# Attention groups kept together on TensorE, a block's outputs finished in the next block, and a new order in the last pair

## The chip, the cores and the metric

The kernel runs on one core of a Trainium2 chip. The core has a matrix engine (TensorE, in profiles PE, with its weight loads as PEld), a vector engine (VectorE, DVE), a scalar engine (ScalarE, ACT), GpSimd (POOL) and SyncE (SP), which here only issues DMAs. Each engine runs its own list of instructions in order, and they meet through semaphores. TensorE writes to a small memory of eight banks, PSUM, from which VectorE and ScalarE read; the rest lies in SBUF. The metric is the time of one execution on the device in microseconds. The figure for a kernel is the median of its timed runs.

## The reference, cut to what matters

The input x is 32 x 64 x 512, the context has the same shape, and all is float32. The first layer is cross attention in which the 64 rows are the channels: a row of 512 is cut into 8 heads of 64, the projections are 64 x 64 matrices that act on the channel axis, and the scores are 64 x 64 for each batch entry and head.

```python
x = x + attention(layernorm(x), ctx, ctx)      # per head: softmax(q k^T / 8) v, then Wo and bo
h = layernorm(x)
gate = silu(h @ dequant(gate_w))               # 512 -> 1792
up   = h @ dequant(up_w)
x = x + (gate * up) @ dequant(down_w)          # 1792 -> 512
```

`dequant` subtracts an integer zero point and multiplies by a scale, both per group of 128 rows and per column. All three weights are integers from 0 to 15.

## The kernel before

Two batch entries side by side make a "pair" of 128 rows, so there are 16 pairs. Four pairs make a block of 512 columns for the feed-forward part; there are four blocks, numbered 0 to 3 (t). Attention works on sets of two pairs, named after their first pair: 0, 2, 4, ... 14.

Feed-forward. The activations are kept transposed, as a high and a low part (hTh, hTl). For each of 14 columns of weights (f), `gate_up` (L615) multiplies four groups g of gate and up weights with both parts into PSUM tiles pg and pu (L624). ScalarE rescales pg and pu between groups (L634), applies SiLU at the last (L637), VectorE forms h (L640), and GpSimd splits it into hh and hl (L650, L651). `down` (L656) multiplies hh and hl with the down weights (L669, L672), and VectorE adds the product into one of four y tiles (L682); a block's first column is copied to y by ScalarE instead (L680). So a column takes 16 matmuls up and 8 down, each with 512 columns. Two lanes of `gate_up` run side by side.

Attention. The class `Attention` (L337) has one method a step: k, v and q projections, scores, the highest of a row, less (subtract), exp, sums, divide, turn (weights times Wo), weigh (times v), residual, and then a second layer norm and flip (transposition for the feed-forward part). Steps k, v, q, scores, turn and weigh are groups of 64 small TensorE products (64 x 64, in four quarters of the array) or, for v, of 16. Each group writes to a tile of two PSUM banks, of which there is one for all (`two_banks`, L872), shared with the transposes of the finishing steps.

Order. A Python loop (L895) emits the program in rounds, 28 to a block and six more at the end. Each round emits a step of lane 0, the attention steps listed for that round in ROUND_STEPS (L576), a `down` step, a step of lane 1, weights still to be dequantised (or sums of squares for a check of the inputs), finishing steps, and a `down` step. Attention of block t+1 is emitted in the rounds of block t. A planner then gives each engine its order: among the instructions that it holds ready it takes the one that was emitted first, that is, of the best priority. Three means bend this. `tc.manual_schedule` keeps the order of a group's instructions on an engine, but others may come between them. `tc.issue_after(ins)` queues instructions behind a given one on its engine, without waiting for its end. `tc.high_priority()` gives what is emitted inside it the priority of the program's start. The start-up part (the list START) is in a written order on all engines.

Finishing. `finish(t)` (L686) has four steps for a block: load the attention result of two pairs from DRAM into the single tile r (L691); transpose their y on TensorE (L696), add (L699) and store (L700); then the same for the other two pairs. Before the change it is created at round LAG = 6 of block t+1 and advanced in rounds 7, 9 and 11, and for the fourth step in round 5 of the block after; for block 2 that is the very end of the loop. `finish_last` (L703) does the four pairs of block 3 after the loop: 16 transposes (L711), three adds on VectorE (L715), for the last pair a copy on ScalarE (L718) and an add on GpSimd (L719), and stores issued in turn by SP and ScalarE (L720). Then every engine reads a flag (L930) and branches: where the check of the inputs failed, a slow general path would follow. The flag is written by VectorE (L749) about twelve rounds before the end.

Of the kernel before, what the change touches and what calls it, by code (L numbers as in the profile page):

```python
# [9 lines left out]
F32 = mybir.dt.float32  # L10
# [16 lines left out]
def kernel(  # L27
# [41 lines left out]
    nc = tc.nc  # L69
    B, D, L = x.shape  # L70
    I = gate_w.shape[1]
    P = 128
# [3 lines left out]
    LC = L // P  # L76
    NPAIR = B // 2
    PB = 4
    NBLK = NPAIR // PB
    TB = PB * P  # L80
    SET = 2
# [4 lines left out]
    o_rows = out.rearrange("(n b) d l -> (b d) n l", b=2)  # L86
# [7 lines left out]
    flag = keep.tile([1, 1], I32, tag="flag", name="flag")  # L94
    ident = keep.tile([P, P], F32, tag="ident", name="ident")
# [18 lines left out]
    with ExitStack() as fast:  # L114
# [96 lines left out]
        def proj(m: int, b: int) -> bass.AP:  # L211
            return w_T[ts(b, D), (m - b) % 4, :]
# [106 lines left out]
        def top_steps():  # L319
# [9 lines left out]
            for piece in pieces:  # L329
# [3 lines left out]
                nc.gpsimd.tensor_tensor(total[:, :n], total[:, :n], square[:, :n], ALU.add)  # L333
                yield


        class Attention:  # L337

# [64 lines left out]
            def heads(self, part: str, m: int, name: str):  # L403
                pp, quarters = self.quarters(name)
                src = self.by_head(part)
                with self.in_order():
                    for c, b, h in quarters:
                        nc.tensor.matmul(
                            pp[ts(h, HD), b, c, :],
                            src[ts(b, D), c, h, :],  # L410
                            proj(m, b),
                            start=True,
                            stop=True,
                        )
                return pp

            def with_bias(self, part: str, pp: bass.AP, m: int):
# [17 lines left out]
            def v(self):  # L435
                self.pv, _ = self.quarters("pv")
                src = self.by_head("c")
                with self.in_order():
                    for i in range(self.n):
                        for h in range(2):  # L440
                            for b in range(2):
                                nc.tensor.matmul(
                                    self.pv[ts(h, D), b, ts(i, KT), :],
                                    proj(WV, b),
                                    src[ts(b, D), ts(i, KT), h, :],
                                    start=True,
                                    stop=True,
                                )

            def v_out(self):  # L450
                nc.scalar.activation(self.by_bank("v"), self.pv, AF.Identity, bias=bvo[:, 0:1])


            def scores(self):
                self.pss, quarters = self.quarters("pss")
                qT, kT = self.by_bank("q_e"), self.by_bank("k_eT")
                with self.in_order():
                    for c, b, h in quarters:
                        nc.tensor.matmul(
                            self.pss[ts(b, D), h, c, :],  # L460
                            qT[ts(h, HD), b, c, :],
                            kT[ts(h, HD), b, c, :],
                            start=True,
                            stop=True,
                        )

            def highest(self):
                n = self.n * KT
# [31 lines left out]
            def turn(self):  # L500
                self.pe, quarters = self.quarters("pe")
                e = self.by_head("q_e")
                with self.in_order():
                    for c, b, h in quarters:
                        nc.tensor.matmul(
                            self.pe[ts(h, D), b, c, :],
                            e[ts(b, D), c, h, :],
                            proj(WO, b),
                            start=True,
                            stop=True,  # L510
                        )

            def turn_out(self):
                nc.scalar.copy(self.by_bank("k_eT"), self.pe)

            def weigh(self):
                self.po, quarters = self.quarters("po")
                eT, vv = self.by_bank("k_eT"), self.by_bank("v")
                with self.in_order():
                    for c, b, h in quarters:  # L520
                        nc.tensor.matmul(
                            self.po[ts(b, D), h, c, :],
                            eT[ts(h, D), b, c, :],
                            vv[ts(h, D), b, c, :],
                            start=True,
                            stop=True,
                        )

            def residual(self):
                x_heads = self.by_head(self.x)  # L530
# [53 lines left out]
        FINISH_AT = 7, 11  # L584
# [27 lines left out]
        h_hi, h_lo, y_sb, pd_two = {}, {}, {}, {}  # L612
# [73 lines left out]
        def finish(t: int):  # L686

            for a in range(0, PB, SET):
                p = t * PB + a
                r = rows.tile([P, SET, L], F32, tag="r", name=f"r_{p}")  # L690
                nc.sync.dma_start(r, x1_dram[:, p : p + SET, :])  # L691
# [7 lines left out]
                nc.vector.tensor_tensor(r, py, r, ALU.add)  # L699
                nc.sync.dma_start(o_rows[:, p : p + SET, :], r)  # L700
                yield

        def finish_last():  # L703

            t = NBLK - 1
            py = [ps_gu.tile([P, CW], F32, tag="gu", name=f"py_last_{i}") for i in range(2)]
            two = two_banks("py_last")
            py += [two[:, 0, :], two[:, 1, :]]
            for l in range(LC):
                for i in range(PB):  # L710
                    nc.tensor.transpose(py[i][:, ts(l, P)], y_sb[t, l][:, ts(i, P)], ident)  # L711
            for i in range(PB):
                r = xs[(t * PB + i) // SET][:, i % SET, :]
                if i < PB - 1:
                    nc.vector.tensor_tensor(r, py[i], r, ALU.add)  # L715
                else:
                    y = hid.tile([P, TB], F32, tag="g", name="y_last", bufs=2)
                    nc.scalar.copy(y, py[i])  # L718
                    nc.gpsimd.tensor_tensor(r, y, r, ALU.add)  # L719
                (nc.scalar if i % 2 else nc.sync).dma_start(o_rows[:, t * PB + i, :], r)  # L720


        def check_bounds():
# [57 lines left out]
        with (  # L781
# [9 lines left out]
            for p in range(PB):  # L791
                j, i = divmod(p, SET)
# [74 lines left out]
        hid = fast.enter_context(tc.tile_pool(name="hid", bufs=3))  # L867
# [22 lines left out]
        LAG = 6  # L890
# [3 lines left out]
        with ExitStack():  # L894
            for r in range(NBLK * ROUNDS + LAG):  # L895
                t, k = divmod(r, ROUNDS)
                if k == 0:
                    attend = attention_steps(t + 1) if t + 1 < NBLK else iter(())
                if k == LAG and t > 0:
                    finishing = finish(t - 1)  # L900
                next(lanes[0], done)
                advance(attend)
                if r >= LAG:
                    advance(downs)
                if r >= 2:
# [24 lines left out]
    with tc.If(nc.values_load(flag, min_val=0, max_val=1) != 0), ExitStack() as slow:  # L930
# [108 lines left out]
```

## Time and profile before

| | us |
|---|---|
| median of 3 timed runs | 449.24 (447.51 to 450.96) |
| profiled execution | 446.75 |
| its span, first to last instruction | 444.6 |
| TensorE busy in the span | 411.4 (93%) |
| VectorE, ScalarE, GpSimd busy | 327.6, 307.0, 280.3 |
| mean granted TensorE clock | 0.989 |

The profile is of one execution. In its rows a line such as "L624" is a line of the kernel. The names of tiles stand as out<-in, without the numbers of their buffers; "x64" is a count. "idle before <- releaser" tells how long the engine had nothing to do before the row and whose semaphore ended that. Matmuls overlap, so the sum of their lengths is more than the time they take; their starts are the better measure. A "q" behind an engine's name means its sequencer: it issues a DMA, reads a register or waits.

### The profile page before, as it was taken

Reading aid. Unit: us, or ns where it says so; the run is one execution under the profiler, and the core shown is the slowest. Engines: PE = TensorE matmul, PEld = TensorE weight load, DVE = VectorE, ACT = ScalarE, POOL = GpSimd, SP = SyncE. Lnnn points to the kernel's source line nnn. Section 1 sums busy time; section 2 is a strip of 40 time slices with the busy share of each in tenths; the row PEclk is TensorE's granted clock in tenths of the full one; section 3 lists DMA queues with packets and bytes.
Section 4 is the critical chain, followed back from the end, with each engine's and each line's share of the span. In section 5 each row is a group of like instructions: output and inputs, shape, how many; then the busy total and the mean of one; then the engine's idle time right before and its main releaser. Section 6 shows DMA issues by size and latency. Waiting matters only on the chain.

```text
span 444.6 us, 10356 instructions
## 1 busy us (share of the span) xinstructions
PE 411.4 (93%) x4191; PEld 316.2 (71%) x4191; DVE 327.6 (74%) x514; ACT 307.0 (69%) x469; POOL 280.3 (63%) x292
## 2 busy tenths in 40 slices
PE   3878979989989999999999999989999999999991
PEld 3656657757768776887788786867778888887871
DVE  4998486896779873895779884896868645668673
ACT  2243886855957589676978589666788787777750
POOL 4384876746844546575778668665787878883311
PEclk9999998999999999999999999999999999999996
DMA  6299585295011200411010102400010012100004
GB/s 210 61 304 369 190 278 150 92 276 177 2 49 49 96 2 0 129 64 50 0 49 1 50 20 77 137 7 1 1 49 2 1 61 83 47 1 0 1 2 149
DMA packets 20912, 36.55 MB, mean 82 GB/s; under 512 B 1832, under 2 KB 7416, under 8 KB 20856
## 3 DMA queue, kind: packets, MB, share of 16 engines
q1 hardware_dynamic: 14056, 24.20, 16.0%
q0 software_dynamic: 6192, 11.01, 8.4%
q8 instruction: 35, 0.57, 0.5%
q10 hardware_dynamic: 608, 0.59, 0.4%
q14 instruction: 21, 0.17, 0.1%
HBM read 27.37 MB, written 8.42 MB: 81 GB/s over the span
## 4 chain that ended last, share of the span: by engine, by line
PE 55%; POOL 17%; issue 11%; DVE 10%; ACT 2%; DMA 2%; ACTq 0%; POOLq 0%; DVEq 0%
PE pu L624 15%; PE pg L624 14%; PE pd L669 8%; PE pd L672 7%; POOL hl L651 5%; POOL squares L333 4%; POOL squares L331 3%; POOL hh L650 2%; DVE y L682 2%; DVE xn_set L112 1%; POOL q_e_set L496 1%; DMA w_nat<-in_L_xattn_Wo_dram 1%; DMA z<-z_dram 1%; DVE q_e_set L473 1%; DVE nd L301 1%
## 5 line engine op out<-in xcount | busy, mean ns | idle before, releaser
L682 DVE SCALAR_TENSOR_TENSOR y<-pd,s_all,y 128x512 f32<-128x512 f32 x204 | 150.5, 743 | 45.8 <-PE pd L672 43.2
L634 ACT ACTIVATE pg<-pg,s_q 128x512 f32<-128x512 f32 x168 | 111.5, 665 | 74.4 <-PE pg L624 73.0
L634 ACT ACTIVATE pu<-pu,s_q 128x512 f32<-128x512 f32 x168 | 110.7, 659 | 5.8 <-PE pu L624 5.6
L669 PE MATMUL pd<-hh,nd 128*128 128x512 f32 x224 | 93.4, 417 | 4.1 <-DVE y L678 2.0
L650 POOL CAST hh<-h 128x512 fp32r<-128x512 f32 x55 | 35.7, 649 | 97.6 <-DVE h L640 93.4
L624 PE MATMUL pg<-hTh,ng 128*128 128x512 f32 x224 | 90.4, 403 | 2.5 <-DVE hTl L567 1.6
L624 PE MATMUL pu<-hTh,nu 128*128 128x512 f32 x224 | 90.5, 404 | 2.3 <-POOL nu L310 2.0
L624 PE MATMUL pu<-hTl,nu 128*128 128x512 f32 x224 | 89.5, 399 | 0.0
L624 PE MATMUL pg<-hTl,ng 128*128 128x512 f32 x224 | 89.0, 397 | 0.0
L672 PE MATMUL pd<-hl,nd 128*128 128x512 f32 x224 | 88.8, 397 | 0.0
L651 POOL TENSOR_TENSOR hl<-h,hh 128x512 fp32r<-128x512 f32 x55 | 72.1, 1311 | 4.3
L640 DVE SCALAR_TENSOR_TENSOR h<-pu,s_all,g 128x512 f32<-128x512 f32 x56 | 41.8, 747 | 29.5 <-ACT g L637 21.4
L333 POOL TENSOR_TENSOR squares<-squares 128x512 f32<-128x512 f32 (+1 forms) x46 | 55.0, 1196 | 1.6
L669 PEld LDWEIGHTS pd<-hh,nd 128*128 128x128 f32 x224 | 42.0, 188 | 19.8 <-DVE y L682 4.9
L624 PEld LDWEIGHTS pg<-hTh,ng 128*128 128x128 f32 x224 | 42.3, 189 | 15.2 <-issue 3.2
L624 PEld LDWEIGHTS pu<-hTh,nu 128*128 128x128 f32 x224 | 42.3, 189 | 14.2 <-POOL nu L310 2.5
L624 PEld LDWEIGHTS pu<-hTl,nu 128*128 128x128 f32 x224 | 42.4, 189 | 9.8 <-issue 0.4
L624 PEld LDWEIGHTS pg<-hTl,ng 128*128 128x128 f32 x224 | 42.2, 189 | 9.5
L637 ACT ACTIVATE g<-pg,s_all 128x512 f32<-128x512 f32 x56 | 38.7, 692 | 14.0 <-PE pg L624 12.4
L672 PEld LDWEIGHTS pd<-hl,nd 128*128 128x128 f32 x224 | 42.3, 189 | 7.9
L310 POOL TENSOR_TENSOR ng<-ng,z 128x512 fp32r<-128x512 f32 (+1 forms) x16 | 16.5, 1039 | 3.4 <-DMA z<-z_dram 3.4
L310 POOL TENSOR_TENSOR nu<-nu,z 128x512 fp32r<-128x512 f32 (+1 forms) x16 | 16.9, 1057 | 2.1 <-DMA nu<-in_L_ffn_up_w_dram 2.0
(293 smaller groups left out, 473.2 us busy)
## 6 DMA issues: line engine op xcount, KB each, us to landing
c_set<-in_ctx_dram SPq DMA_DIRECT2D x6, 512.0 KB
x<-in_x_dram SPq DMA_DIRECT2D x6, 512.0 KB
z<-z_dram SPq DMA_DIRECT2D x6, 512.0 KB
ng<-in_L_ffn_gate_w_dram POOLq DMA_DIRECT2D x3, 1024.0 KB, 6.7
nu<-in_L_ffn_up_w_dram POOLq DMA_DIRECT2D x3, 1024.0 KB, 9.0
x_dram<-x SPq DMA_DIRECT2D x6, 512.0 KB
r<-x_dram SPq DMA_DIRECT2D x6, 512.0 KB
out_dram<-r SPq DMA_DIRECT2D x6, 512.0 KB
```

Source lines behind the costliest of these rows:

```text
L310: nc.gpsimd.tensor_tensor(piece, piece.bitcast(F32), z16[:, m, g, :], ALU.subtract)
L331: nc.gpsimd.tensor_tensor(square[:, :n], piece, piece, ALU.mult)
L333: nc.gpsimd.tensor_tensor(total[:, :n], total[:, :n], square[:, :n], ALU.add)
L624: nc.tensor.matmul(acc, w[:, g, ts(f, P)], half[:, g, :], start=(g == 0 and half is hi), stop=(g == KT - 1 and half is lo), skip_group_che ...
L634: nc.scalar.activation(acc, acc, AF.Copy, scale=by)
L637: nc.scalar.activation(g_sb, acc, AF.Silu, scale=by)
L640: ins = nc.vector.scalar_tensor_tensor(h_sb, acc, by, g_sb, ALU.mult, ALU.mult)
L650: nc.gpsimd.tensor_copy(hh, h_sb)
L651: ins = nc.gpsimd.tensor_tensor(hl, h_sb, hh.bitcast(F32), ALU.subtract)
L669: nc.tensor.matmul(pd, w, h_hi[t, f], start=(t, f) != LAST, stop=False, skip_group_check=True)
L672: nc.tensor.matmul(pd, w, h_lo[t, f], start=False, stop=True, skip_group_check=True)
L682: ins = nc.vector.scalar_tensor_tensor(y, pd, by, y, ALU.mult, ALU.add)
```

## The change

It has three parts. First, a new context `in_one_piece` takes the place of the plain written order in the six group steps of Attention, for sets of two pairs, and is put around the transposes of `finish`. It keeps the order as before, and after the group's first product it raises the priority of the rest. Second, `finish(t-1)` is created at round 5 rather than 6, so its four steps fall in rounds 5, 7, 9 and 11 of one block. Third, in `finish_last` ScalarE's copy of the last pair is emitted ahead of the adds, and the stores that ScalarE issues are queued behind it; the read of the flag is emitted before `finish_last`, and what `finish_last` gives ScalarE and GpSimd is queued behind those engines' reads.

```diff
+        @contextmanager
+        def in_one_piece(rush: bool = True):
+            with tc.manual_schedule(engines={mybir.EngineType.PE}), ExitStack() as ahead:
+                yield lambda: ahead.enter_context(tc.high_priority()) if rush else None
...
             def in_order(self):
-                return tc.manual_schedule(engines={mybir.EngineType.PE})
+                return in_one_piece(self.n > 1)
...
-                with self.in_order():
+                with self.in_order() as first_taken:
                     for c, b, h in quarters:
                         nc.tensor.matmul(
...
                         )
+                        first_taken()
...
                 py = two_banks(f"py_{p}")
-                for i in range(SET):
-                    for l in range(LC):
-                        nc.tensor.transpose(
-                            py[:, i, ts(l, P)], y_sb[t, l][:, ts(a + i, P)], ident
-                        )
+                with in_one_piece() as first_taken:
+                    for i in range(SET):
+                        for l in range(LC):
+                            nc.tensor.transpose(
+                                py[:, i, ts(l, P)], y_sb[t, l][:, ts(a + i, P)], ident
+                            )
+                            first_taken()
...
+            y = hid.tile([P, TB], F32, tag="g", name="y_last", bufs=2)
+            copied = nc.scalar.copy(y, py[PB - 1])
             for i in range(PB):
                 r = xs[(t * PB + i) // SET][:, i % SET, :]
                 if i < PB - 1:
                     nc.vector.tensor_tensor(r, py[i], r, ALU.add)
                 else:
-                    y = hid.tile([P, TB], F32, tag="g", name="y_last", bufs=2)
-                    nc.scalar.copy(y, py[i])
                     nc.gpsimd.tensor_tensor(r, y, r, ALU.add)
-                (nc.scalar if i % 2 else nc.sync).dma_start(o_rows[:, t * PB + i, :], r)
+                with tc.issue_after(copied.ins):
+                    (nc.scalar if i % 2 else nc.sync).dma_start(o_rows[:, t * PB + i, :], r)
...
-                if k == LAG and t > 0:
+                if k == FINISH_AT[0] - 2 and t > 0:
                     finishing = finish(t - 1)
...
-        finish_last()
-    with tc.If(nc.values_load(flag, min_val=0, max_val=1) != 0), ExitStack() as slow:
+        n_traced = len(nc.cur_bb.bb.instructions)
+        other = nc.values_load(flag, min_val=0, max_val=1)
+        with ExitStack() as behind:
+            for ins in nc.cur_bb.bb.instructions[n_traced:]:
+                if ins.engine in (mybir.EngineType.Activation, mybir.EngineType.Pool):
+                    behind.enter_context(tc.issue_after(ins))
+            finish_last()
+    with tc.If(other != 0), ExitStack() as slow:
```

More of the change, by code (lines that the diff above doesn't have):

```diff
@@ L437, in v @@
                 src = self.by_head("c")
-                with self.in_order():
+                with self.in_order() as first_taken:
                     for i in range(self.n):
@@ L456, in scores @@
                 qT, kT = self.by_bank("q_e"), self.by_bank("k_eT")
-                with self.in_order():
+                with self.in_order() as first_taken:
                     for c, b, h in quarters:
@@ L465, in scores @@
                         )
+                        first_taken()
             def highest(self):
@@ L502, in turn @@
                 e = self.by_head("q_e")
-                with self.in_order():
+                with self.in_order() as first_taken:
                     for c, b, h in quarters:
@@ L511, in turn @@
                         )
+                        first_taken()
             def turn_out(self):
@@ L518, in weigh @@
                 eT, vv = self.by_bank("k_eT"), self.by_bank("v")
-                with self.in_order():
+                with self.in_order() as first_taken:
                     for c, b, h in quarters:
@@ L527, in weigh @@
                         )
+                        first_taken()
             def residual(self):
@@ L693, in finish @@
                 py = two_banks(f"py_{p}")
-                for i in range(SET):
-                    for l in range(LC):
-                        nc.tensor.transpose(
-                            py[:, i, ts(l, P)], y_sb[t, l][:, ts(a + i, P)], ident
-                        )
+                with in_one_piece() as first_taken:
[4 more added lines that the diff above has]
+                            )
+                            first_taken()
                 nc.vector.tensor_tensor(r, py, r, ALU.add)
```

## The prediction

> **What bounds the kernel now.** I read the page's first part, then TensorE's timeline, then the tail.
>
> ```profile
> PE 411.4 (93%) x4191; PEld 316.2 (71%) x4191; DVE 327.6 (74%) x514; ACT 307.0 (69%) x469; POOL 280.3 (63%) x292
> ```
>
> TensorE is the busiest, but a busy share says little where matmuls overlap: one 128x512 matmul is recorded at 0.39 us and the next starts 0.23 us later. So I counted starts. The 1344 feed-forward matmuls at 0.2333 us make 313.6 us; they run from 39.7 to 433.0. The rest is attention, transposes and what is lost between. The timeline of TensorE shows an attention group that was cut up (start, length, engine, line, operation, tiles, shape, count):
>
> ```profile
> 168.86 0.33 PE L505 MATMUL pe_8to<-w_T,q_e_set 64*64 64x64 f32 x4 [0.60 <-POOL q_e_set L496]
> 169.12 0.50 PE L624 MATMUL pu<-hTh,nu 128*128 128x512 f32 x1
> 169.46 0.40 PE L624 MATMUL pu<-hTl,nu 128*128 128x512 f32 x1
> 169.78 0.33 PE L505 MATMUL pe_8to<-w_T,q_e_set 64*64 64x64 f32 x2
> 170.04 0.50 PE L669 MATMUL pd<-hh,nd 128*128 128x512 f32 x1
> 170.38 0.40 PE L672 MATMUL pd<-hl,nd 128*128 128x512 f32 x1
> ```
>
> and one that ran whole:
>
> ```profile
> 226.06 0.40 PE L624 MATMUL pu<-hTl,nu 128*128 128x512 f32 x1
> 226.38 1.16 PE L521 MATMUL po_10to<-v_set,k_eT_set 64*64 64x64 f32 x64
> 227.47 0.49 PE L669 MATMUL pd<-hh,nd 128*128 128x512 f32 x1
> 227.81 0.40 PE L672 MATMUL pd<-hl,nd 128*128 128x512 f32 x1
> ```
>
> A piece of two costs 0.32 (feed-forward start to piece) + 0.26 (169.78 to 170.04) + 0.34 (to the next start) = 0.92 us, against 2 x 0.23 = 0.47 without it and 0.03 for its own two products (64 take 1.28 us net of the same 0.47, so one is about 0.013 once 0.42 is set aside). Each cut thus costs 0.42 us.
>
> TensorE's timeline has eight cut groups in blocks 0 to 2: pk_4 in 3 pieces, pss_4 in 2, pq_6 in 3, pe_6 in 2, pe_8 in 6, pe_10 in 2, pe_12 in 5, pe_14 in 2. That is 17 cuts: 6 before 122 us, 11 after.
>
> In one stretch ScalarE sets the pace beside it (columns of the view of windows: stretch, its length, busy PE, PEld, DVE, ACT, POOL, clock, DMA):
>
> ```profile
> 162.13:173.40 11.27, 10.67 (x88) 6.88 (x87) 5.58 (x10) 11.21 (x16) 6.83 (x7) 1.00 0.00 0
> ```
>
> ScalarE has no idle moment here (the exponential, two table loads, four copies of y); pe_8 lies in it, and pe_12 in its twin from 262.6. After 343 there is no attention. The tail:
>
> ```profile
> 433.36 1.22 DVE L699 TENSOR_TENSOR r<-py,r 128x1024 f32<-128x1024 f32 x1
> 434.49 0.74 DVE L682 SCALAR_TENSOR_TENSOR y<-pd,s_all,y 128x512 f32<-128x512 f32 x1
> 435.65 1.89 DVE L715 TENSOR_TENSOR x<-py_last,x 128x512 f32<-128x512 f32 x3 [0.42 <-PE py_last L711]
> 436.97 0.36 ACTq L720 DMA_DIRECT2D out_dram<-x  x1
> 437.57 0.58 ACT L718 COPY y_last<-py_last 128x512 f32<-128x512 f32 x1 [5.91 <-DVE x L715]
> 438.23 1.26 POOL L719 TENSOR_TENSOR x<-y_last,x 128x512 f32<-128x512 f32 x1 [12.54 <-DMA out_dram<-x]
> 439.52 0.34 ACTq L720 DMA_DIRECT2D out_dram<-x  x1
> ```
>
> The third block's last add (L699, 1.22 us) stands ahead of the last y. ScalarE's copy waits behind its own DMA issue of pair 1 (436.97), though its transposes were done at 435.93. From the last issue to the end of the span it is 444.6 - 439.5 = 5.1 us.
>
> **Part one: groups in one piece.** It removes up to 17 x 0.42 = 7.1 us of TensorE time and adds nothing. Two rules of the Trainium skill disagree on this. "TensorE: Matmul & The Clock Gate" (Step-by-step) says that weight loads are pulled ahead of running matmuls, which would make a cut nearly free: saving 0. "TensorEngine Tiling (Array Packing)" (Key Properties) says that a change of tiling mode drains the array; with the recorded length for the drain (0.39 against a pitch of 0.23, twice per piece) that makes 0.32 a cut, 5.4 us in all. The tile view of pe_8 has, under idle time before its weight loads,
>
> ```profile
>   issue: 1.8, 5
> ```
>
> five entries of about 0.36 us: the loads were not pulled ahead. I take the row's 0.42.
>
> How much of it is kept? The 6 early cuts (2.5 us) are on the chain of waits, which runs through pk_4's pieces, DVE h at 56.76 and the z load at 58.14, and near 122 through POOL hh, hl and nu. Those are released by TensorE's work, so most carries over: I take 2.0 (bounds 0 and 2.5). The 9 cuts of pe_8 and pe_12 (3.8 us) lie where ScalarE is full; ScalarE waits for TensorE again only from 173.4 on, so part of the time comes back as waiting for it: 2.7 (bounds 0.8 and 3.8). The cuts of pe_10 and pe_14 (0.8) have no such neighbour: 0.8. Sum 5.5. The feed-forward matmuls displaced by a whole group wait at most 1.09 us, as they do now for 28 of the 36 groups.
>
> **Part two: outputs a block sooner.** The finishing steps go from rounds 7, 9, 11 and 5 of the next block to 5, 7, 9, 11. For each half one load, eight transposes, one add and one store are the same as before. One set leaves the tail and one is added to block 1. There the eight transposes cost 0.79 + 0.08 us on TensorE, mostly beside the full ScalarE: -0.4 (bounds 0 and -0.9). The add needs 1.22 us of VectorE in round 7, where VectorE stands idle for 4.0 us (to 170.74, for ScalarE's g); without that cover pe_8 would start up to 1.2 + 0.75 us later, as it needs the same two banks. po_8 and po_12 no longer wait 0.4 for such an add; I leave that as reserve. On SP's queue the load in round 5 comes behind the context load of round 3. The second load, round 9, passes ahead of the residual's store (round 10); the second store, round 11, goes ahead of the row load of round 13, which then waits for an add two rounds earlier than itself: no cost. POOL's queue is not passed by any of it.
>
> In the tail the last y starts at 433.37 (the pitch of y is 0.67 us) rather than 434.49: 1.1 us.
>
> **Part three: the copy first, the flag read early.** With y 1.1 us earlier the transposes end at 434.83, the copy follows at 434.85 to 435.43, GpSimd adds until 436.77, and ScalarE issues the last store at 436.8 instead of 439.52: 2.7 us, of which 1.1 is part two's. The store of pair 1 fits between copy and last issue. VectorE's third add ends at 436.44, so it is not the later one. After that come landing, SP's row of waits and the closing barrier, the 5.1 us. That SP went idle 3.2 us after its branch (437.99 to 441.19) moves along; I keep 2.2 of the 2.7 for the end (bounds 1.1 and 2.7), since landings after a branch may lag.
>
> The flag's readers now stand ahead of this:
>
> ```profile
> L930 POOLq TENSOR_LOAD <-flag x1: 945/945/945, 438.2 to 438.2; - x1
> L930 ACTq TENSOR_LOAD <-flag x1: 480/480/480, 439.9 to 439.9; - x1
> ```
>
> Behind ScalarE's read are queued the copy and two stores; behind GpSimd's the last add. The flag is written at 410.8; GpSimd is idle from 425.7, ScalarE from 431.66 to the copy, so they should hide. Should they fall among the feed-forward steps, ScalarE has 24 x 0.2333 - 7 x 0.57 = 1.6 us free per column of weights, against 0.48. I charge 0.3 (bounds 0 and 1.4, both reads in full). The start-up groups run under a complete written order and are not touched: 0.
>
> **Sum.** 5.5 - 0.4 + 2.2 - 0.3 = 7.0 us. The profiled execution took 446.75 (span 444.6 and 2.15 around it); it becomes 439.7. The median of the timed runs is 2.49 higher, 449.24, so 442.2.
>
> **Rivals.** *The cuts fill waits.* If TensorE's pieces stood in time that it would have waited anyway for ScalarE, VectorE or POOL, only pe_10, pe_14 and the tail are left: 0.8 - 0.4 + 2.2 - 0.3 = 2.3, 446.9. For it: the full ScalarE, the 2.2 us waits at 62 and 122.7. Against: within pe_8 hardly any gap between starts exceeds the switch.
>
> *It doesn't do what it says.* Raised priority only ranks what is ready; if the planner holds the next product of a group as not ready when it picks, pieces remain. Then 1.5 is left: 447.7. Against: groups of 62 and 64 in a row exist now.
>
> *Slower: the second reload.* Both halves share one buffer r, so the second load starts only when the first store has landed. SP's timeline:
>
> ```profile
> 281.82 0.38 SPq L700 DMA_DIRECT2D out_dram<-r  x1
> 284.61 0.33 SPq L691 DMA_DIRECT2D r<-x_dram  x1
> ```
>
> 2.8 us, plus about 4.0 for 512 KB (estimated from 220 GB/s of two transfers in the stretch from 284.6 to 288.8): 6.8 us between adds. Today's closest pair stands 12 us apart (transposes at 359.8 and 371.9). If the new order puts the second add within 3 us of the first, VectorE, which issues in order, is held 3.8 us, y and h behind it, then TensorE: 3 x 3.8 = 11.4, giving 453.6. It outweighs the gain from 2.3 us a block, a spacing under 4.5 us. Against: the add is queued behind the newest feed-forward step of its round.
>
> **How the numbers follow.** Forecast 0.58 (own range 439.4 to 445.3: all terms at their best, or the early cuts and the tail at their lower bounds), cuts fill waits 0.18, pieces remain 0.10, reload 0.10, other new orders 0.04. The runs before scatter by 0.4% to either side, and 1% (4.5 us) is about what a measurement can tell from no change. The range goes from all bounds at their best (7.1 + 2.7 = 9.8, 439.4, less 1.5 of scatter) to the second rival with scatter: 438.0 to 449.2. Faster 0.62, same 0.26, slower 0.12.
>
> **What would show it.** Every attention group as one row of 64 (or 16); no "issue" entries inside pe_8; py pairs in rounds 7 and 11 and none after 400; L718 starting within 0.1 us of the last transpose; the last store 2.7 us sooner against the last y's pitch. I am wrong if TensorE's gaps grow in 160 to 180 and 260 to 280, if L699 shows a wait for a DMA, or if the flag reads stand before L634 steps that TensorE waits for.

## The result and the profile after

The changed kernel takes 443.99 us (median of 4 runs, 443.15 to 445.11) against 448.77 (447.51 to 450.96) for the kernel before beside it. The ratio is 0.989, with a 95% interval of 0.9844 to 0.9936: 4.8 us less, where 7.0 were forecast (442.2, range 438.0 to 449.2). The two profiled executions happen to lie closer together than that, 446.75 and 445.11, so a single pair of traces is not enough to place the gain. The table further down puts the traces of all experiments side by side.

First the page's busy times of the changed kernel:

```profile
PE 406.4 (92%) x4191; PEld 313.2 (71%) x4191; DVE 332.9 (75%) x514; ACT 306.1 (69%) x469; POOL 279.5 (63%) x292
```

TensorE is busy 5.0 us less with as many matmuls; ScalarE, which is the second limit where pe_8 lies, has what it had. TensorE's timeline around that place, and VectorE's, both of the changed kernel (start, length, engine, line, operation, tiles, shape, count, idle before):

```profile
165.79 1.04 PE L709 MATMUL py<-ident,y 128*128 128x128 f32 x8
...
170.84 0.50 PE L636 MATMUL pg<-hTh,ng 128*128 128x512 f32 x1 [1.21 <-ACT g L649]
...
174.01 1.16 PE L515 MATMUL pe_8to<-w_T,q_e_set 64*64 64x64 f32 x64
```

```profile
170.88 0.75 DVE L652 SCALAR_TENSOR_TENSOR h<-pu,s_all,g 128x512 f32<-128x512 f32 x1 [4.01 <-ACT g L649]
171.54 1.21 DVE L713 TENSOR_TENSOR r<-py,r 128x1024 f32<-128x1024 f32 x1
```

pe_8 runs as one row of 64 products, as every other attention group of blocks 0 to 2 now does. It also runs 5.1 us later than before (174.01 against 168.86). The transposes py took the two banks at 165.79; the add that frees them (L713) stands on VectorE behind h, which waits 4.01 us for ScalarE's g. The kernel before has the same wait, but nothing queued behind it that holds the banks:

```profile
170.74 0.75 DVE L640 SCALAR_TENSOR_TENSOR h<-pu,s_all,g 128x512 f32<-128x512 f32 x1 [4.01 <-ACT g L637]
```

In the changed kernel the add ends at 172.75; up to 174.01 TensorE's order has feed-forward matmuls ahead of pe_8. TensorE itself now waits 1.21 us for the same g, a time in which the kernel before had pieces of pe_8 to run.

The tail of the changed kernel:

```profile
430.81 2.15 DVE L694 SCALAR_TENSOR_TENSOR y<-pd,s_all,y 128x512 f32<-128x512 f32 x3
432.35 1.53 PE L725 MATMUL py_last<-ident,y 128*128 128x128 f32 x12 [0.41 <-DVE y L694]
433.59 1.89 DVE L732 TENSOR_TENSOR x<-py_last,x 128x512 f32<-128x512 f32 x3 [0.64 <-PE py_last L725]
433.91 0.58 ACT L728 COPY y_last<-py_last 128x512 f32<-128x512 f32 x1 [3.37 <-PE py_last L725]
434.57 1.26 POOL L734 TENSOR_TENSOR x<-y_last,x 128x512 f32<-128x512 f32 x1 [10.02 <-ACT y_last L728]
434.91 1.30 ACTq L736 DMA_DIRECT2D out_dram<-x  x2
```

ScalarE copies 0.03 us after the last transpose (its first row ends at 433.88), and its second store is issued at 435.87 (the row of two begins at 434.91), against 439.52 before. But from there to the end of the span it is now 7.1 us, where it was 5.1. The order in the tail came as written, and the end hardly moved: from the last feed-forward start to the end it is 11.90 us (431.11 to 443.01), against 12.04 before (432.61 to 444.65).

In the table the span of each profiled execution (in us) is cut at feed-forward starts: from the 1st to the 337th (early, where attention's start-up group and the last unpacking of weights lie), to the 1233rd (middle, with pe_8 to pe_14), to the 1344th, and from there to the end (tail). Ahead of the first start lie another 38.7 to 40.3 us. The kernels below the line of after are the experiments. The middle repeats well: 253.0 in the four kernels with the changed kernel's middle (after, again, after_short, all_sp), 254.3 in the three with that of before. The early part doesn't: it scatters by 1.5 us and more among like kernels.

| kernel | early | middle | last 112 | tail | span |
|---|---|---|---|---|---|
| before | 111.3 | 254.3 | 27.3 | 12.0 | 444.6 |
| after | 111.9 | 253.0 | 27.0 | 11.9 | 443.0 |
| again (after, once more) | 111.5 | 253.0 | 27.0 | 12.0 | 442.4 |
| p1_groups | 112.0 | 250.8 | 27.3 | 12.1 | 442.0 |
| p2_sooner | 113.1 | 255.6 | 27.0 | 11.2 | 445.5 |
| p3_tail | 112.8 | 254.3 | 27.3 | 11.9 | 446.6 |
| late | 110.9 | 252.2 | 27.8 | 11.9 | 442.0 |
| y_dve | 110.6 | 249.9 | 26.9 | 11.2 | 438.7 |
| before_ydve | 112.8 | 251.8 | 27.3 | 12.3 | 443.2 |
| p1_ydve | 110.9 | 251.5 | 27.3 | 12.1 | 441.5 |
| before_short | 111.8 | 254.3 | 27.3 | 10.3 | 443.2 |
| after_short | 111.0 | 253.0 | 26.9 | 8.4 | 438.9 |
| early_cut | 115.3 | 250.5 | 27.3 | 12.9 | 445.0 |
| all_sp | 111.0 | 253.0 | 27.0 | 12.0 | 442.4 |

### The profile page after: what moved, and what is told of

It is laid out like the page before. It is cut to its first block, busy times and chain, and to the rows that moved or that the text cites. A ratio compares the mean times of both kernels' runs of the same rounds, so it can differ in the third digit from the quotient of the medians.

```text
span 443.0 us, 10348 instructions
## 1 busy us (share of the span) xinstructions
PE 406.4 (92%) x4191; PEld 313.2 (71%) x4191; DVE 332.9 (75%) x514; ACT 306.1 (69%) x469; POOL 279.5 (63%) x292
## 4 chain that ended last, share of the span: by engine, by line
PE 54%; POOL 16%; DVE 11%; issue 10%; ACT 5%; DMA 2%; POOLq 0%; ACTq 0%; DVEq 0%
PE pu L636 15%; PE pg L636 15%; PE pd L681 8%; PE pd L684 7%; POOL hl L663 4%; POOL squares L333 3%; POOL squares L331 3%; POOL hh L662 2%; DVE y L694 2%; DVE nd L301 2%; DVE xn_set L112 1%; DVE q_e_set L483 1%; DMA x<-in_x_dram 1%; ACT pg L646 1%; ACT pu L646 1%
## 5 line engine op out<-in xcount | busy, mean ns | idle before, releaser
L646 ACT ACTIVATE pg<-pg,s_q 128x512 f32<-128x512 f32 x168 | 111.3, 664 | 72.1 <-PE pg L636 70.4
L663 POOL TENSOR_TENSOR hl<-h,hh 128x512 fp32r<-128x512 f32 x55 | 71.7, 1303 | 4.3
L652 DVE SCALAR_TENSOR_TENSOR h<-pu,s_all,g 128x512 f32<-128x512 f32 x56 | 41.8, 747 | 29.8 <-ACT g L649 23.3
```

Source lines behind the costliest of these rows:

```text
L646: nc.scalar.activation(acc, acc, AF.Copy, scale=by)
L652: ins = nc.vector.scalar_tensor_tensor(h_sb, acc, by, g_sb, ALU.mult, ALU.mult)
L663: ins = nc.gpsimd.tensor_tensor(hl, h_sb, hh.bitcast(F32), ALU.subtract)
```

## The experiments

A gain below is (1 - ratio) x 448, with the ratio to the kernel before on the same chip.

### Each part alone

**again** is the changed kernel once more, on the chip of the next three.

> The changed kernel once more, for a second profile and a firmer ratio. If the measured gain is real and not the draw of the runs, 4 to 5.5 us under the kernel before on the same chip, with ScalarE's g again ending a wait of about 1.4 us at 169 and at 270. If the gain is a draw, under 3 us.

Measured: 443.47 us, ratio 0.9901 (0.9868 to 0.9934), a gain of 4.4.

**p1_groups** keeps only part one; `LAG` and `finish_last` are those of before.

```diff
             def in_order(self):
-                return tc.manual_schedule(engines={mybir.EngineType.PE})
+                return in_one_piece(self.n > 1)
...
```

> Part one alone: groups in one piece, finishing steps and tail as before. The prediction's sum gives 5.5 us under before. If most cuts only filled waits for ScalarE, VectorE and GpSimd (rival), 0.8 to 2.5 us under before, and the waits of 1.4 us for ScalarE's g at 169 and 270 are there.

Measured: 443.56 us, ratio 0.9899 (0.9878 to 0.9919), a gain of 4.5. Part one alone has the whole gain. Its pe_8 starts where it did before, and the only thing it waits for is GpSimd, 0.6 us:

```profile
169.74 1.16 PE L515 MATMUL pe_8to<-w_T,q_e_set 64*64 64x64 f32 x64 [0.60 <-POOL q_e_set L506]
```

Cut at every 56 feed-forward starts, the two traces show where the middle's 3.5 us lie. Against before, the stretch of pe_8 (five cuts gone) is 1.83 us shorter, that of pe_12 (four) 1.24, those of pe_10 and pe_14 (one each) 0.39 and 0.38. The rest of the middle agrees within 0.02 us, but for 0.35 lost ahead of pk_14, which early_cut below doesn't lose. So a cut was worth 0.31 to 0.39 us, also where ScalarE is full. The two stretches with a lone cut are 0.36 to 0.41 shorter in each of the other kernels with whole groups but late, which puts transposes there.

**p2_sooner** keeps only part two.

```diff
-                if k == LAG and t > 0:
+                if k == FINISH_AT[0] - 2 and t > 0:
                     finishing = finish(t - 1)
```

> Part two alone: finishing steps from round 5. The prediction gives 0.7 us under before (1.1 in the tail less 0.4 in block 1). If the code fetch after the last branch sets the end, the tail's 1.1 still counts, since the last store and the branch move together: 0.5 to 1.1. If the transposes stand in TensorE's way at round 7, within 0.5 of before or slower.

Measured: 448.71 us, ratio 1.0018 (1.0004 to 1.0032): 0.8 us slower, where a gain was expected. By the table the tail is 0.85 us shorter, near the 1.1 expected, the last 112 are 0.4 shorter and the middle is 1.3 longer. These cancel, so the traces don't place the 0.8 us. This middle isn't that of the changed kernel either: without part one the first transposes in block 1 and in block 2 are cut too, into six pieces (from 166.53 to 169.56 in block 1), while pe_8 and pe_12 fall into three pieces each.

**p3_tail** keeps only part three.

```diff
+            y = hid.tile([P, TB], F32, tag="g", name="y_last", bufs=2)
+            copied = nc.scalar.copy(y, py[PB - 1])
             for i in range(PB):
...
+                with tc.issue_after(copied.ins):
+                    (nc.scalar if i % 2 else nc.sync).dma_start(o_rows[:, t * PB + i, :], r)
...
```

> Part three alone: the copy first, the flag read early. The prediction gives 1.3 us under before (2.2 less what part two gives, less 0.3 for the reads, and 0.5 of ScalarE's read after its last store). If the fetch of code after the branches grows when they come together (4.5 us in the changed kernel against 3.0 to 3.2 before), 0 to 0.5.

Measured: 447.56 us, ratio 1.0001 (0.9978 to 1.0024): nothing, and a tail of 11.95 us in the trace against 12.04.

Part one thus makes the gain, part two costs a little, part three does nothing that can be measured. By the traces parts two and three make the middle 2.2 us longer (253.0 against 250.8). The times of again and p1_groups, 443.47 and 443.56, don't show that. The rest asks why.

### Part two: where the sooner outputs hurt

**late** puts the finishing steps of the changed kernel farther back in the block.

```diff
-        FINISH_AT = 7, 11
+        FINISH_AT = 11, 22
```

> All three parts, but the finishing steps in rounds 9, 11, 20 and 22, so that the first transposes come after weigh and not between less and turn. Theory (the transposes of round 7 hold the two banks until VectorE's add, so pe comes 5 us late and no longer fills TensorE's wait for ScalarE's g): the waits of 1.4 us at 169 and 270 go and the middle is 2 us shorter, 441.5 to 442.5 where the changed kernel has 443.5. Rival (the added transposes and adds cost their own time wherever they stand): 443 to 444.

Measured: 443.97 us, ratio 0.9903 (0.9868 to 0.9939): no better than the changed kernel, as the rival in the expectation had it. In its trace pe_8 does start at 168.0 again and TensorE's waits for g beside it are gone, but the middle is only 0.8 us shorter (252.2), still 1.3 above p1_groups. A wait of 1.38 us ahead of pk_10 stays. The changed kernel has it too (1.37 us), and there VectorE's timeline shows it:

```profile
192.94 2.68 DVE L112 TENSOR_SCALAR xn_set<-x,mv_10to,rs_10to 128x512 f32<-128x512 f32 x2 [0.17 <-PE ph_8to L556]
195.54 0.74 DVE L694 SCALAR_TENSOR_TENSOR y<-pd,s_all,y 128x512 f32<-128x512 f32 x1
196.21 1.21 DVE L579 TENSOR_TENSOR hTl<-ph_8to,hTh 128x1024 fp32r<-128x1024 f32 x1
```

and not in p1_groups, whose timeline of VectorE at that place is

```profile
192.72 0.54 DVE L112 TENSOR_SCALAR xn_set<-x,mv_10to,rs_10to 128x512 f32<-128x512 f32 x1
...
194.16 1.22 DVE L579 TENSOR_TENSOR hTl<-ph_8to,hTh 128x1024 fp32r<-128x1024 f32 x1
```

hTl (L579) frees the two banks for pk_10. In p1_groups one xn_set of set 10 (L112) stands shortly ahead of it and takes 0.54 us. In the changed kernel two do, and the pair takes 2.68 us: the first starts 0.07 us after GpSimd's hl (L663, from 192.87, 1.29 us), the second beside GpSimd's squares (L331, from 194.12, 1.22 us). So hTl starts 3.27 us after the first xn_set and not 1.44. p2_sooner has the same two kinds of wait, 1.06 us for g and 1.37 ahead of pk_10, and the kernel before has neither. Part two moved more than the steps it names: it gave the planner another order on VectorE here too. It isn't alone in that: before_ydve below, without part two, has both xn_set in a row and waits 1.45 us ahead of pk_10.

### ScalarE's load in the middle

In **y_dve** the first column's y of blocks 1 to 3 is made by VectorE and not by ScalarE, in the changed kernel: 12 copies, recorded at 0.68 to 0.73 us each, off a ScalarE that is full where eight of them lie.

```diff
-                elif (t, f) == (0, 0):
-                    nc.vector.tensor_scalar(y, pd, by, None, ALU.mult)
                 elif f == 0:
-                    nc.scalar.activation(y, pd, AF.Copy, scale=by)
+                    nc.vector.tensor_scalar(y, pd, by, None, ALU.mult)
```

> The changed kernel with the first column's four products of every block copied to y by VectorE, as block 0 does, not by ScalarE. Theory (TensorE waits at 169 and 270 because ScalarE is full): ScalarE has 4 x 0.57 = 2.3 us less to do in each of these stretches, the waits of 1.4 us go, 2 to 3 us under the changed kernel. Rival (VectorE sets the pace once it has four more steps of 0.74): no gain or a loss of up to 2.

Measured: 440.64 us, ratio 0.9836 (0.9795 to 0.9878). It is faster than the kernel before, and by the point estimates some 3 us faster than the changed one too, though the intervals overlap (again: 0.9868 to 0.9934). The page shows the load moved from ScalarE (306.1 to 300.2) to VectorE (332.9 to 340.7):

```profile
PE 404.3 (92%) x4191; PEld 311.8 (71%) x4191; DVE 340.7 (78%) x526; ACT 300.2 (68%) x457; POOL 280.4 (64%) x292
```

TensorE's waits for g at 170 and 270 are gone, and the middle is 249.9, 3.1 us shorter than the changed kernel's.

**before_ydve** makes the same edit in the kernel before.

> The kernel before with the first column's copies of y on VectorE in every block. If ScalarE's full stretch costs TensorE time only where a wait for g is seen (the cuts fill it in the kernel before), 0 to 1 us under before. If the relief is worth the same with cut groups as it was in the changed kernel, 3 us under before.

Measured: 444.95 us, ratio 0.9931 (0.9905 to 0.9957), a gain of 3.1; the middle is 251.8, 2.5 shorter. That is the 3 us expected for a relief of ScalarE, but not for that reason alone, since the edit also took cuts away: pe_8 lies in 3 pieces rather than 6 and pe_12 in one rather than 5, so that 4 cuts of the middle's 11 are left. Three cuts at 0.37 us and four at 0.31, the values of p1_groups, make 2.3 us (an estimate) of the middle's 2.5; what the lighter ScalarE adds to that goes, by the stretches, for the new wait ahead of pk_10. What the full ScalarE by itself cost the kernel before isn't shown.

**p1_ydve** makes it in p1_groups.

> Part one and the copies of y on VectorE, finishing steps and tail as before. Part two's late pe and its wait for ScalarE are both absent here, so the relief of ScalarE has less to give than in the changed kernel: 441.5 to 443, against 440.6 for the changed kernel with the same edit. If the two edits add up, 440.5.

Measured: 442.32 us, ratio 0.9869 (0.9831 to 0.9907), a gain of 5.9 (4.2 to 7.6), where the two gains by themselves add to 4.5 + 3.1 = 7.6. By the point estimates 1.7 us of the two are the same time; that isn't clear of noise. before_ydve gives it a reason: seven cuts are gone there before part one removes any.

The profile of p1_ydve holds a disturbance. Its granted clock is 0.89 from 290 to 305 us, where p1_groups, before_ydve and y_dve have 1.00, and the 56 starts there take 1.5 us more than in before_ydve, with the same wait of 1.75 us ahead of pk_14 in both. Without it the middle would be 249.9 us (an estimate), which is what y_dve has. So with ScalarE relieved, parts two and three cost the middle nothing, where without the edit the changed kernel's is 2.2 longer than p1_groups'. The ratio of y_dve, 0.9836, is below p1_ydve's, but the intervals overlap, so that parts two and three are a gain there isn't settled.

### Part three: what stands behind the last store

**after_short** and **before_short** leave out the slow general path behind the flag (a one-column memset stands in its place), in the changed kernel and in the kernel before. The branch then passes over next to no code.

```diff
     with tc.If(other != 0), ExitStack() as slow:
-        const = slow.enter_context(tc.tile_pool(name="f_const", bufs=1))
...
+        work = slow.enter_context(tc.tile_pool(name="f_work", bufs=1))
+        none = work.tile([P, 1], F32, tag="none", name="f_none")
...
```

> The changed kernel with the slow general path left out (a memset stands in it), so that the branch at the end jumps over almost nothing. Theory (the end waits for code fetched after the branch, 4.5 us on SP and ScalarE): these engines go on 0.1 to 0.5 us after their branch, the end comes at the landing of the last store plus 2.2 us, about 1.5 us sooner than in the changed kernel. Rival (landings set the end): no change.

> The kernel before with the slow general path left out in the same way. Theory: ScalarE no longer joins late, but the last store is issued at the same place and its landing and SP's row of waits remain: 0 to 0.5 us under before; from the last feed-forward start to the end it is then 1.5 to 2.5 us longer than in the changed kernel without the path, where with it the two differ by 0.1.

Measured: after_short 440.75 us, ratio 0.9836 (0.979 to 0.9883); before_short 445.17 us, ratio 0.9942 (0.9916 to 0.9968). The tails are 8.43 and 10.27 us. Without the code behind the branch the change's tail is 1.84 us shorter than the old one, against 0.14 with it: the order of parts two and three does its work, and what comes with the slow path takes it back. The edit did more than empty the branch, though. It moved the branches ahead of the last stores (in after_short SP's to 410.1 us and ScalarE's to 429.2, in before_short to 435.4 and 431.3) and left SP 11 waits after its last store in place of 20. In both short kernels the end follows the landing of the last store, at 437.9 and 442.1 us, by 1.0 and 1.1 us. The times don't confirm this by themselves: the two short versions lie 4.4 us apart, the two full ones 4.8, and each difference is uncertain by some 2 us.

What stands there is seen in the view of the branch's line. The COMPARE_BRANCH of SP or ScalarE takes some 0.05 us, but the engine's next instruction comes much later. Kernel before (duration three times in ns, then first and last start):

```profile
L930 SPq EVENT_SEMAPHORE  x8: 17/17/17, 441.2 to 443.0; - x8
...
L930 SPq COMPARE_BRANCH  x1: 45/45/45, 437.9 to 437.9; - x1
...
L930 ACTq COMPARE_BRANCH  x1: 58/58/58, 440.5 to 440.5; - x1
...
L930 ACTq EVENT_SEMAPHORE  x1: 17/17/17, 443.5 to 443.5; - x1
```

Changed kernel:

```profile
L953 SPq EVENT_SEMAPHORE  x8: 17/17/17, 440.8 to 441.3; - x8
...
L953 SPq COMPARE_BRANCH  x1: 45/45/45, 436.2 to 436.2; - x1
L953 ACTq COMPARE_BRANCH  x1: 58/58/58, 436.2 to 436.2; - x1
...
L953 ACTq EVENT_SEMAPHORE  x1: 17/17/17, 440.8 to 440.8; - x1
```

Before, SP resumed 3.2 us after its branch and ScalarE, which branched 2.5 us later, 3.0 us after its own. In the changed kernel both branch within 0.03 us and both resume 4.5 us later. In before_short SP goes on 0.14 us after its branch. What passes meanwhile is in the view of DMA traffic. In the changed kernel, from the branches to the resumption (436.24 to 440.80 us), it has five packets of the kind "instruction" (queue: packets, MB, share of the time of 16 DMA engines):

```profile
q14 instruction: 4, 0.03, 1.9%
q8 instruction: 1, 0.02, 1.5%
```

In the kernel before there are three in SP's wait and four in ScalarE's. before_short has none from SP's branch to the end, after_short one from ScalarE's (429.2) on. So code is fetched while these engines stand behind their branches; which packet lets which engine go, the view doesn't tell. The trace's finer times split the stretch from the last store's issue to the end: before 0.99 (issue, flag read, branch) + 3.02 (ScalarE resumes) + 1.12 (closing) = 5.13; after 0.40 + 4.53 + 2.21 = 7.14. The last term grew because SP has two rows of waits, 20 in all, to pass, 1.3 us, before it can close. Before, SP had all but four of them behind it when ScalarE resumed (its last begins at 443.71, ScalarE resumes at 443.53); now SP resumes as late as ScalarE.

**all_sp** takes the two branches apart: SP issues all four last stores.

```diff
-                    (nc.scalar if i % 2 else nc.sync).dma_start(o_rows[:, t * PB + i, :], r)
+                    nc.sync.dma_start(o_rows[:, t * PB + i, :], r)
```

> The changed kernel, but SP issues all four stores of the last block, so that ScalarE has nothing after its copy and takes its branch at about 434.5 us of the span, some 2 us ahead of SP (in the changed kernel both branch at 436.2 and both resume 4.5 us later). Theory that two branches taken at the same moment hold each other up: ScalarE resumes about 3.0 us after its branch, SP issues its last store at 436.0 to 436.2, branches at about 436.6 and resumes 3.0 to 3.3 us after that, at 439.7 rather than 440.8; the end comes about 1.1 us sooner, so from the last feed-forward start to the end of the span some 10.8 us against 11.9, and the median is some 1.1 us under the changed kernel's (about 442.9 against 444.0). Rival, that the resumption is held up by the stores in flight at that moment, or has another cause that does not lie in ScalarE's branch: SP resumes 4.1 to 4.6 us after its branch, at 440.7 to 441.2, and the time is that of the changed kernel or up to 0.4 us longer.

Measured: 444.32 us, ratio 0.9919 (0.9897 to 0.994), no gain. The view of the branch's line, all_sp:

```profile
L953 SPq EVENT_SEMAPHORE  x8: 17/17/17, 440.0 to 440.8; - x8
...
L953 ACTq COMPARE_BRANCH  x1: 50/50/50, 433.2 to 433.2; - x1
...
L953 ACTq EVENT_SEMAPHORE  x1: 17/17/17, 436.1 to 436.1; - x1
L953 SPq COMPARE_BRANCH  x1: 45/45/45, 436.6 to 436.6; - x1
```

SP's resumption takes 3.3 us with ScalarE's branch out of the way (and ScalarE's 2.8), so the first theory holds for the wait itself; the stores in flight did not keep it at 4.5. The expected 1.1 us did not come because four issues in a row take SP 2.9 us: it branches 6.2 us after the last feed-forward start, not 5.1. The tail is 12.0 again. How near two branches must lie is not settled: in p3_tail they are 0.36 us apart and the waits 3.3 and 3.4, in y_dve 0.25 apart and 4.1 and 4.3. The other engines branch in the same microseconds, and no run keeps their branches apart.

### The early cuts

**early_cut** is p1_groups with the groups of sets 4 and 6 left as before, so that the six early cuts come back and the eleven later ones do not.

```diff
             def in_order(self):
-                return in_one_piece(self.n > 1)
+                return in_one_piece(self.n > 1 and self.p >= 2 * PB)
```

> Part one alone, but only for sets from 8 on: the six cuts of sets 4 and 6 remain. The prediction held 2.0 us for these six: then 445.5 or 2 us over part one alone (443.5). The traces of the runs so far (feed-forward starts 1 to 337: 111.3 us with whole groups in the mean, 112.3 with cut ones) say about 1: 444 to 445. If the cuts are filled by other waits there: no more than 0.3 over part one alone.

Measured: 444.55 us, ratio 0.9915 (0.9882 to 0.9947), a gain of 3.8 where p1_groups has 4.5: the six cuts are worth 0.7 us, with an uncertainty of 1.7 that excludes neither 0 nor the forecast's 2.0. The traces say more. Cut at every 112 feed-forward starts, the second stretch takes 36.2 us in all six kernels with the early pieces and 35.3 or 35.4 in all eight with whole groups: the two cuts of pq_6 there give their 0.84 in full. The third takes 36.4 in five of the six and 34.9 in the kernel before, against 35.1 to 35.8 with whole groups. In those five the granted clock is 0.91 from 116 to 136 us; in the kernel before and in all eight with whole groups it is 1.00. So this is no measure of pe_6's one cut: the fall of the clock, with the same cuts, is worth 1.5 us. Just ahead of it TensorE waits for nu, 2.03 to 2.06 us in the six and 1.37 to 1.42 in the eight. That whole groups keep the clock up through this shorter wait is a possibility that no run tests (the kernel before waits 2.04 and keeps its clock), but part of the measured gain may be this. The first stretch, with the three cuts of pk_4 and pss_4 (1.3 us), takes 39.3 to 42.7 with pieces (median 40.2) and 39.9 to 41.5 without (median 40.3): no gain. Timelines of VectorE and TensorE in the changed kernel show what took its place:

```profile
64.85 4.93 DVE L301 TENSOR_TENSOR nd<-nd,z 128x512 fp32r<-128x512 f32 x4
```

```profile
70.56 0.50 PE L681 MATMUL pd<-hh,nd 128*128 128x512 f32 x1 [1.99 <-DVE y L694]
```

Four unpacking steps of the down weights stand in a row ahead of a y that TensorE waits for. In the kernel before, TensorE waits 2.05 us at the same stage, for a y behind a load of zero points (L301 starts at 62.22, after 1.38 us for the load). In early_cut that load was later still and the wait 4.9. In these traces the weights set the end of this stage; that TensorE's saved time ahead of it goes into the wait fits the first stretch, which isn't shorter with whole groups.

## Why the prediction was right, and where it was wrong

The result lies in the range and on the predicted side, 1.8 us above the predicted time. The range was wide: it holds the times of the rivals "the cuts fill waits" (446.9) and "pieces remain" (447.7) as well, so lying in it says little. What shows the main step right is p1_groups. Against the steps of the sum (5.5 - 0.4 + 2.2 - 0.3 = 7.0):

**0.42 us a cut, eleven cuts in the middle: right.** 2.7 + 0.8 = 3.5 were forecast, and the middle of p1_groups is 3.5 us shorter than that of before. The parts fit less well than the sum. The lone cuts of pe_10 and pe_14 gave 0.39 and 0.38 us, so the 0.42 is a little high and the 0.32 from the recorded lengths too low; that a cut would be nearly free is out. pe_8's five gave 1.83, as much for each as a lone one, and pe_12's four 1.24: together 3.1 against 2.7, so most of the 1.1 taken off for the full ScalarE was not needed. A loss of 0.35 ahead of pk_14, not foreseen, brings the sum back to 3.5; that it agrees to the tenth is luck. The rival that the cuts fill waits (0.8 of it) falls.

**Early cuts, 2.0: too large.** The step that failed is that the waits on that chain "are released by TensorE's work, so most carries over". For the start-up group's three cuts they are not: a load of zero points and the unpacking on VectorE set that stage. The chain had shown the z load by name. What the runs support is 0.8 for pq_6, nothing for the first three, and 0.7 (uncertain by 1.7) for all six by time; pe_6's one stays open.

**Part two, -0.4 in the block and +1.1 in the tail: wrong in size and, as a sum, in sign.** Alone it costs 0.8 us (0.2 to 1.4). The tail's share is there when part two is alone (0.85). The failed step is that the add "needs 1.22 us of VectorE in round 7, where VectorE stands idle for 4.0 us". That idle time was not free: VectorE was waiting in h (L652) for ScalarE, and the add is queued behind h. The price named for the lost cover was 1.2 + 0.75 us on pe_8; it was 5.1, since the banks stay taken for the whole wait and TensorE's order adds 1.3 us. The other new order, two xn_set ahead of hTl, was not foreseen at all. That ScalarE's load is the larger cause is what y_dve and p1_ydve speak for: with it relieved, parts two and three no longer lengthen the middle, though the wait ahead of pk_10 stays (1.38 us; p1_ydve has 0.83 there without part two).

**The tail, 2.2 of 2.7: the order right, the end wrong.** Measured from the last feed-forward start, the last store is issued 2.15 us sooner (4.76 us after it, was 6.91), against 2.7. What failed is "after that come landing, SP's row of waits and the closing barrier, the 5.1 us": taken as one block that moves along. It holds a resumption after a branch for each engine and a row of waits on SP, which ran beside each other before and stand in line now. The prediction saw the 3.2 us after SP's branch and let it "move along". It was 4.5, and the gain of the tail is 0.1 us by the traces (2.2 forecast, bound 1.1).

**Flag reads, 0.3: not needed.** GpSimd's read starts at 423.2 and ScalarE's at 429.2, both under 0.5 us. The steps around them follow at their usual pace (GpSimd's hl starts 0.08 us after hh ends, ScalarE's next L688 0.58 us after the one before). That they no longer stand in the tail is the 0.6 us by which the first term above fell from 0.99 to 0.40.

**The other rivals.** Every group is one row, so "it doesn't do what it says" falls. VectorE's L713 shows no wait for a DMA, so the second reload is no matter (its 4.0 us for the load was short: two loads of 512 KB at 220 GB/s together take 4.8, but nothing rests on it). The signs named as proof of an error, gaps of TensorE that grow in 160 to 180 and 260 to 280, did come (1.2 us for ScalarE's g in each): they came with part two (p1_groups has neither), not from a failure of part one.

By the runs, the sum reads 3.5 for the middle of part one and about 0.8 early, less 0.8 (by time, alone) to 1.9 (by the changed kernel's middle and last 112) for part two, and 0.1 for the tail: 2.5 to 3.6. The measured 4.8 is uncertain by about 2, so it agrees; up to 1.5 us may come from the granted clock between 116 and 136 us, which isn't settled.

## What to carry to other kernels

Idle time of an in-order engine ahead of an instruction that waits is no room for a step that will be queued behind that instruction; ask instead what the new step holds (here two PSUM banks) until the wait ends. The end of a kernel is not one constant block: each engine's branch and each row of waits starts when that engine is through, so moving the last engine forward pays only until the next one, and two that arrive together may both be slower. Where TensorE and a second engine are both full, relieving the second engine is worth trying early: moving 12 small copies off ScalarE brought 3.1 us in the old kernel, in part because fewer groups were cut, and carried the new one to 440.64.

## What the runs showed of the hardware that was not expected

- A branch over the long slow path delays the next instruction of SP or ScalarE by 2.8 to 3.5 us. Where the two branch within 0.25 us of each other it is 4.1 to 4.6 us, in all four such profiles (after, again, late, y_dve). With the path left out it was 0.14 us for SP in before_short. In these waits the DMA view counts packets of code.
- VectorE's xn_set took 0.54 us where it started 0.18 us before GpSimd's hl (p1_groups; hl then took 1.52 us), and 1.50 us where it started 0.07 us after it (changed kernel; hl took 1.29).
- The last store was not what the end waited for: in the changed kernel it has landed at 439.3, 1.5 us before SP and ScalarE resume. With the path left out the end does follow its landing (437.9 and 438.9 in after_short).
- The granted clock fell to 0.91 over 20 us of the early part in five of six profiles with cut early groups and in none of eight with whole ones; that made 1.5 us.
